# The channel shift of a convolution block by transfers, and two elementwise steps moved from VectorE to ScalarE, in a kernel that follows a table of times

## The chip, the cores and the metric

The kernel runs on one core of a Trainium2 chip. A core has a matrix engine (TensorE, PE in the profile, with its weight loads as PEld), VectorE (DVE), ScalarE (ACT), GpSimd (POOL), and SyncE (SP), which here only issues transfers. The engines run side by side, each through its own queue in order, and wait for each other by semaphores. The metric is the time of one execution on the device in microseconds, as the median of several runs.

## The reference

The input is 64 images of 96 channels and 56 x 56 pixels in float32. Two layers follow each other.

The first is a convolution block. An expansion by a 1x1 convolution to 192 channels, with a batch norm and a silu; a shift of four quarters of the channels by one pixel each, up, left, down and right, with zeros at the edge; a shuffle of the channels; a depthwise 3x3 convolution with batch norms and a scaled identity added; silu; a squeeze-and-excite gate; a projection back to 96 channels; the input added; silu.

```
up, left, down, right = shift of x0, x1, x2, x3 by one pixel
out = shuffle(concat(up, left, down, right))
dw  = depthwise3x3(out)
out = silu(bn(dw + bn(out * id_w)))
```

The second treats each image as 3136 tokens of 96 channels. It adds an attention-like part (layer norm, a matmul to 192 channels with relu, a Fourier transform over the tokens, a complex scale and relu, the inverse transform, a matmul back to 96) and then a feed-forward part (layer norm, then two linear layers whose inputs and weights are rounded to an 8-bit float with 2 bits of mantissa, and whose sums and biases are rounded to a 16-bit float).

## The kernel before

Everything is done image by image, and several images are under way at once. The kernel is a set of small step functions, each of which issues a few instructions: `ea_mm` and `ea_ev` for the expansion of the first 128 channels, `eb_mm` and `eb_ev` for the last 64, `dw_mm`, `gt` and `lt` for the depthwise convolution, `pj_*` for the projection, `c_*` and `sp_*` for the first norm, `w1_*`, `f1_*`, `f2_*`, `w2_*`, `i1_*` and `i2_*` for the Fourier part, `n_*` for the second norm, `x_*`, `h_*` and `o_*` for the feed-forward part, and `x_in`, `f1_st`, `f2_ld`, `i1_st`, `i2_ld` and `o_st` for transfers. The suffix tells the kind: mm a matmul on TensorE, ev its copy out of PSUM, st and ld transfers.

The order of the work is set by hand, by a table. `PLAN` has a time for every step of one image, and `PERIOD` (104.415) is the distance of one image from the next. The steps of all images are sorted by `b * PERIOD + time` and issued in that order (L1021). So the table gives only the order: each engine's queue holds its instructions in that order, and when one really starts depends on its queue and its waits. Part numbers belong to a step: `lt0` to `lt8` are the nine taps.

The shift and the last 64 channels. `xi` holds one image with a border of one pixel, and one more row of ones that carries the bias. For the first 128 channels a quarter is 32 output channels wide, so `ea_mm` reads a window of `xi` that is already shifted (`window`, L394). For the last 64 channels a quarter is only 16 wide. There `eb_mm` (L423) uses weights padded with zeros, `ex_b`, and adds two matmuls of 32 channels in PSUM, one for each shift. The result goes to `e_b`, whose 128 partitions are two halves of the image times 64 channels; four groups have 7 rows in each half and a fifth has the one row that each half needs of the other. `eb_ev` (L439) applies the silu on ScalarE and writes `e_b`. The nine `lt` (L501) then do the depthwise taps of these channels on VectorE, on 1568 elements a partition, and `gt` (L488) does the same for a part of the first 128 channels; TensorE does the rest of these with diagonal weights (`dw_mm`).

The Fourier part and its limits. The matmuls of `w1`, `f1`, `f2`, `w2`, `i1` and `i2` take turns on two PSUM buffers of 1024 columns (`mix_ps`, L385), all other matmuls on four smaller ones (`psb`). `w1_ev` and `f2_s` on VectorE, and `f1_ev`, `f2_u`, `w2_ev` and `i1_ev` on ScalarE, read the large buffers and set when they come free. The spectrum goes through DRAM twice: `f1_st` and `f2_ld`, then `i1_st` and `i2_ld` (L894), each on SP's queue; `i2_mm` (L908) starts when the rows are back.

The second norm: `n_mm` gives the centred values in PSUM, `n_sq` squares them on ScalarE, `n_v` sums on VectorE, `n_pow` takes the inverse root on GpSimd, and `n_x` (L939) multiplies, on VectorE, and writes `xt` as 8-bit floats for `x_mm`. `o_b` (L994) adds the last bias to the 16-bit result in place, on VectorE, and `o_f` on GpSimd adds the residual.

Of the kernel before, what the change touches and what calls it, by code (L numbers as in the profile page):

```python
# [7 lines left out]
F32 = mybir.dt.float32  # L8
F16 = mybir.dt.float16
F8 = mybir.dt.float8e5  # L10
AF = mybir.ActivationFunctionType
# [4 lines left out]
C = 96  # L16
# [29 lines left out]
    "x_in": (-38.1521383, -39.0313507, -38.1421592, -29.5328898, -31.2956739, -49.0488434, -53.4484414),  # L46
    "ea_mm": (12.0718742, -17.6347537, -10.7617034, 21.5633635, 22.3815668, -27.4838656, 20.8444028),
    "ea_ev": (12.7625155, -16.7409792, -10.2350254, 22.8295655, 23.1485054, -26.8731307, 22.1730006),
    "eb_mm": (-24.9502373, -30.5666300, -24.2855462, -28.5828763, -25.9329880),
    "eb_ev": (-24.4007802, -29.0870142, -23.6123341, -27.8995689, -24.6078971),  # L50
    "dw_mm": (23.4012692, 25.8065649, 27.7186515),
    "dw_ev": (27.9416140, 28.2430920, 28.7919300, 27.9867333),
    "gt": (
        23.2893122, 23.6403008, 24.7084475, 26.2430594, 26.9625479, 31.2412715, 31.4805021, 31.6854971, 32.2081696,
    ),
    "gs": (35.5837667,),
    "lt": (
        -22.5058312, -19.2781395, -16.0020596, -8.0830315, -5.6296105, 10.1142041, 11.3886298, 19.2795806, 21.4543236,
    ),
    "ls": (25.2835963,),  # L60
    "se1_mm": (37.8386681,),
    "se1_ev": (39.1563442,),
    "se2_mm": (42.2104890,),
    "se2_ev": (42.5090105,),
    "se2_th": (42.5348385,),
    "se2_pw": (44.5599295,),
    "pj_mm": (49.5318932, 49.8734317, 59.5185874, 59.7120461),
    "pj_add": (56.4058332, 52.4986738, 55.7518604, 50.5578889, 62.0059751, 61.7026537, 60.4028988, 62.1927170),
    "pj_ev": (57.4207106, 54.3789408, 55.8536804, 52.2030223, 63.6733108, 63.8836718, 63.6259052, 62.6258470),
    "c_mm": (64.0752216, 64.2093635, 64.1823953, 67.0833950, 66.7447747, 69.5982071, 72.4532417),  # L70
    "c_st": (65.0824106, 67.4206134, 66.4132179, 72.2682213, 68.2606423, 72.6061913, 77.5871617),
    "c_v": (75.0177019, 80.2993483),
    "c_pow": (76.9880774, 83.3522602),
    "sp_v": (79.7136264, 84.6589124),
    "sp_ld": (81.9540079, 100.3604366),
    "sp_mm": (82.7320710, 85.1331094),
    "sp_ev": (83.1910055, 89.2419308),
    "sp_st": (84.0313823, 91.2838064),
    "w1_mm": (87.1292398, 87.4650255, 98.3635707, 98.4934935, 110.6216463, 107.9122279, 120.0467391, 121.3099629),
    "w1_ev": (88.4753488, 89.6606871, 101.8145979, 102.1457936, 112.1440653, 108.1905137, 121.3097887, 122.6670408),  # L80
    "f1_mm": (92.4329783, 93.9413197, 102.1475205, 103.0182652, 113.5623380, 116.3511041, 124.4090057),
    "f1_ev": (93.7039784, 97.4318585, 105.1183982, 107.7539289, 114.5573476, 117.0384673, 125.0694061),
    "f1_st": (95.0609843, 107.1692695, 108.9817725, 116.6729491, 117.5442084, 123.9939344, 131.9160193),
    "f2_ld": (133.6363282, 134.4630140, 140.6697451, 148.5715304),
    "f2_mm": (134.0425675, 147.3297886, 141.4082867, 149.2531837, 154.9429947, 160.6005067),
    "f2_u": (
        135.7660808, 139.9328971, 150.0014492, 150.1774566, 142.0370395, 143.6677530, 151.8678977, 153.2265284,
        158.0769692, 158.2232886, 163.0150847, 163.7461056,
    ),
    "f2_s": (  # L90
        139.9838717, 141.9248308, 152.1198117, 152.1631925, 146.0651549, 146.9747432, 153.1711643, 153.5938621,
        158.8634913, 158.8771759, 163.4341277, 164.8079993,
    ),
    "f2_r": (144.0109778, 153.5991704, 148.7491184, 156.4744876, 159.5323121, 167.3989389),
    "f2_p": (147.3373312, 156.4376915, 150.8056372, 162.7962275, 161.2485624, 169.6535678),
    "w2_mm": (162.8750213, 159.0401908, 167.8463641, 170.9122124),
    "w2_ev": (166.1738607, 159.3392453, 169.9047276, 172.9202964),
    "i1_mm": (166.2532752, 170.2567201, 173.3466199),
    "i1_ev": (169.8622129, 169.2534145, 172.5737063, 172.7147615, 173.4172382, 175.8838783),
    "i1_st": (176.0044405, 181.5692360, 182.6172474),  # L100
    "i2_ld": (184.2359480, 189.7575058),
    "i2_mm": (189.1909858, 188.5912958, 198.3815920, 196.3644526),
    "i2_ev": (190.1672752, 191.7878315, 189.7544042, 190.0259385, 201.9647931, 201.2712574, 197.5328114, 196.9362029),
    "n_mm": (194.1130474, 192.8787732, 204.8582159, 214.9114818, 204.2743160, 208.7914968, 202.7409001),
    "n_sq": (194.2312052, 193.7168380, 207.3352049, 215.2880641, 204.5888294, 211.0101067, 204.2114539),
    "n_v": (195.8071958, 194.1326641, 207.9103855, 215.6737355, 210.6800138, 211.1668257, 205.1116119),
    "n_pow": (199.0696775, 198.6534423, 208.5806040, 217.6340298, 211.4651491, 211.6665408, 205.2342939),
    "n_x": (200.9444099, 200.0782994, 210.9942246, 218.2272324, 212.2097752, 217.7795795, 206.6554285),
    "x_mm": (202.3277533, 200.8863307, 217.5496343, 219.8683239, 216.0782138, 219.4636355, 207.7029227),
    "x_ev": (203.0727144, 205.8355865, 217.8646967, 220.1867695, 218.5087841, 220.9334171, 210.6012880),  # L110
    "h_mm": (
        222.6648803, 228.7422803, 227.1038383, 222.6083835, 226.7371014, 221.6336581, 240.2108454, 244.1922873,
        250.9628025, 264.7686132, 241.4045277, 261.6477397, 239.3650273, 275.9040589, 273.9147053, 281.5223325,
        289.5279227, 292.6649548, 292.9723382, 304.6785521, 295.5712479,
    ),
    "h_ev": (
        226.6852415, 230.3656128, 228.5097649, 225.3267902, 228.0507042, 222.0383113, 242.5456463, 246.3460033,
        252.6763911, 265.6097590, 254.2998624, 262.5612295, 246.1430109, 277.5023560, 275.1846881, 283.9585886,
        293.1805221, 293.5958189, 301.7720564, 306.3205803, 300.5311760,
    ),  # L120
    "h_b": (
        227.9255047, 233.9060669, 232.2385810, 225.3989664, 230.2401387, 225.1796682, 244.0448546, 246.4021124,
        262.6890256, 267.2414236, 271.8809825, 274.9000227, 256.1324325, 278.4500149, 275.7375432, 293.7448928,
        297.6207746, 299.0605055, 302.8303038, 319.7169921, 312.2914909,
    ),
# [14 lines left out]
def conv_attn_ffn(  # L140
# [98 lines left out]
    for e in range(2):  # L239
        nc.vector.tensor_copy(  # L240
            ex_b[:, e, :, e, :], ex_w[:, 128:MID].rearrange("p (u e i) -> p u e i", u=2, e=2)[:, :, e, :]
        )
# [956 lines left out]
```

## Time and profile before

| | |
|---|---|
| median of 3 runs | 6730.21 us (6729.68 to 6732.37) |
| the profiled execution | 6725.7 us |
| its span, first to last instruction | 6723.9 us |
| PE busy | 6152.3 us, 91% |
| VectorE busy | 5639.2 us, 84% |
| ScalarE busy | 4384.5 us, 65% |
| GpSimd busy | 1493.4 us, 22% |
| mean granted TensorE clock | 0.986 |
| moved by DMA | 689.44 MB, 103 GB/s |

A row of a group reads: line, engine, operation, names of output and inputs, shapes, count, then the busy time in us and the mean of one in ns, then the time that the engine stood idle just before it and what ended that. A matmul in float32 shows as two records. A row of a timeline reads: start, length, engine, line, operation, and in brackets the idle time before it. A row of an SP timeline shows only the issue of a transfer, not its landing. A row of the table of windows has the window, its length, the busy time and count of each engine, the granted clock, the share of the DMA engines and GB/s.

### The profile page before, as it was taken

To read this page: it belongs to the slowest core of one execution; us is meant where nothing else is said; L and a number is where in the kernel's file an instruction comes from. 1 tells how busy PE (TensorE), PEld (TensorE's weight loads), DVE (VectorE), ACT (ScalarE), POOL (GpSimd) and SP (SyncE) were. 2 spreads that over 40 slices of the span, in tenths; PEclk is the share of its full clock that TensorE was granted. 3 is DMA by queue.
4 is the path that set the end of the run, shared out by engine and by line. 5 is a ranking of instruction groups with operands and counts; after the bars stand their busy time and mean duration, and the time that the engine had idled before them with its cause. 6 is when DMAs were issued, how large, how long until landed. Compare 5 with 4: busy or idle time off the path is not lost.

```text
span 6723.9 us, 246864 instructions
## 1 busy us (share of the span) xinstructions
PE 6152.3 (91%) x107010; PEld 4033.1 (60%) x107010; DVE 5639.2 (84%) x10903; ACT 4384.5 (65%) x8718; POOL 1493.4 (22%) x1035
## 2 busy tenths in 40 slices
PE   6999999999999999999999999999999999999996
PEld 3656655666656666566566666666665656656654
DVE  7888888888888888888888888888888888888884
ACT  2666666666666666666666666666666666666665
POOL 1212212222222222122222222221222222212212
PEclk9999999999999999999999999999999999999997
DMA  3344444344444444443444444444434444444333
GB/s 76 99 104 106 103 104 105 101 102 109 103 103 105 106 104 103 104 109 98 102 109 103 103 104 106 104 103 104 108 100 103 107 103 103 105 103 108 101 96 82
DMA packets 996378, 689.44 MB, mean 103 GB/s; under 512 B 671298, under 2 KB 944522, under 8 KB 995162
## 3 DMA queue, kind: packets, MB, share of 16 engines
q1 hardware_dynamic: 992570, 671.88, 39.1%
q8 instruction: 841, 13.78, 0.9%
q10 hardware_dynamic: 2720, 1.77, 0.1%
q14 instruction: 247, 2.02, 0.1%
HBM read 329.66 MB, written 341.31 MB: 100 GB/s over the span
## 4 chain that ended last, share of the span: by engine, by line
PE 43%; DVE 35%; ACT 12%; DMA 4%; issue 4%; POOL 1%; SPq 1%; POOLq 0%; ACTq 0%; DVEq 0%
PE ps_d L475 10%; DVE ue L813 6%; DVE buf_h L823 5%; DVE s L810 5%; PE psa L873 5%; ACT ue L794 4%; PE ps_ea L413 4%; PE psa L696 4%; PE ps_eb L430 4%; DVE buf_h L708 3%; DVE d_last L509 3%; PE psa L723 3%; DMA buf_h<-rows 3%; PE ps_c L626 3%; DVE y L974 3%
## 5 line engine op out<-in xcount | busy, mean ns | idle before, releaser
L1002 POOL TENSOR_TENSOR o<-t,o 112x448 f32<-112x448 f32 x448 | 688.7, 1537 | 3539.8 <-DVE o L996 1277.9
L509 DVE SCALAR_TENSOR_TENSOR d_last<-e_b,taps,d_last 128x1568 f32<-128x1568 f32 x512 | 1008.6, 1970 | 2.6
L980 ACT CAST h<-y 128x448 fp8e5<-128x448 f16 x1344 | 747.7, 565 | 167.9 <-DVE y L974 167.8
L496 DVE SCALAR_TENSOR_TENSOR d_vec<-e_a,taps,d_vec 128x1120 f32<-128x1120 f32 x512 | 766.1, 1496 | 13.9
L969 ACT CAST y<-ps_h 128x448 f16<-128x448 f32 x1344 | 692.0, 542 | 90.2 <-PE ps_h L964 79.9
L475 PE MATMUL ps_d<-e_a,diag 32*32 32x504 f32 x18432 | 710.6, 590 | 17.0 <-issue 16.9
L936 POOL TENSOR_TENSOR rs<-v,mhalf 112x4 f32<-112x4 f32 x448 | 450.0, 1012 | 1193.0 <-DVE v L620 1193.0
L696 PE MATMUL psa<-w1c,t 112*64 112x96 f32 x14336 | 652.5, 247 | 1.4 <-ACT fs L735 1.4
L696 PEld LDWEIGHTS psa<-w1c,t 112*64 112x64 f32 x14336 | 607.2, 137 | 73.7 <-DVE t L920 35.9
L794 ACT ACTIVATE ue<-psa,fa 128x448 f32<-128x448 f32 (+1 forms) x512 | 358.9, 704 | 381.3 <-DVE ue L813 355.8
L634 DVE BATCH_NORM_STATS2 st<-ps_c 112x6 f32<-112x96 f32 x1792 | 336.3, 249 | 313.4 <-PE ps_c L626 313.4
L475 PEld LDWEIGHTS ps_d<-e_a,diag 32*32 32x32 f32 x18432 | 392.0, 103 | 325.1 <-issue 69.8
L974 DVE TENSOR_SCALAR y<-y,qb 128x448 f16<-128x448 f16 x1344 | 510.2, 384 | 69.1 <-ACT y L969 65.2
L964 PE MATMUL ps_h<-xq,q 96*128 96x448 fp8e5 x1344 | 425.1, 359 | 131.2 <-ACT t L600 109.3
L769 PEld LDWEIGHTS psa<-l_tab,buf_g 128*64 128x64 f32 x7424 | 361.5, 137 | 241.1 <-issue 109.4
L615 ACT ACTIVATE sq<-ps_n 112x384 f32<-112x384 f32 x448 | 220.2, 492 | 430.6 <-PE ps_n L608 430.2
L769 PE MATMUL psa<-l_tab,buf_g 128*64 128x112 f32 x7424 | 414.6, 263 | 83.8 <-DVE ue L813 46.2
L834 PEld LDWEIGHTS psa<-w2a,buf_h 128*64 128x64 f32 (+1 forms) x7424 | 331.8, 135 | 218.8 <-issue 172.2
L653 POOL TENSOR_TENSOR rs<-v,mhalf 112x16 f32<-112x16 f32 (+1 forms) x128 | 338.0, 2640 | 494.0 <-DVE v L648 494.0
L723 PE MATMUL psa<-buf_h,f_tab 56*64 56x384 f32 x3584 | 401.6, 504 | 47.6 <-DVE buf_h L708 46.8
L810 DVE SCALAR_TENSOR_TENSOR s<-psa,fa,ue 128x448 f32<-128x448 f32 (+1 forms) x512 | 325.1, 635 | 137.3 <-ACT ue L794 137.2
L708 DVE SCALAR_TENSOR_TENSOR buf_h<-psa,rs_full 128x768 f32<-128x768 f32 (+1 forms) x512 | 424.8, 850 | 10.2 <-PE psa L696 9.0
(175 smaller groups left out, 12093.1 us busy)
## 6 DMA issues: line engine op xcount, KB each, us to landing
spec<-fs SPq DMA_DIRECT2D x896, 192.0 KB
buf_g<-spec SPq DMA_DIRECT2D x384, 336.0 KB
buf_h<-rows SPq DMA_DIRECT2D x128, 672.0 KB
x<-in_x SPq DMA_DIRECT2D x896, 84.0 KB
out_dram<-o SPq DMA_DIRECT2D x896, 84.0 KB
rows<-buf_g SPq DMA_DIRECT2D x128, 420.0 KB
rows<-buf_g SPq DMA_DIRECT2D x64, 504.0 KB
buf_g<-spec SPq DMA_DIRECT2D x128, 210.0 KB
```

Source lines behind the costliest of these rows:

```text
L475: nc.tensor.matmul(pss[r][j * 32 : j * 32 + 32], lhsT=diag[pr, tap, :], rhs=e_a[pr, r0 : r0 + SR, dx : dx + HW], start=tap == 0, stop=tap ...
L496: nc.vector.scalar_tensor_tensor(d_vec, win, w, d_vec, ALU.mult, ALU.add)
L509: nc.vector.scalar_tensor_tensor(d_last, win, w, d_last, ALU.mult, ALU.add)
L696: nc.tensor.matmul(ps[hc * 64 : hc * 64 + 64, k, 0:C], lhsT=t[:, n0 : n0 + 64], rhs=w1c[:, hc * C : hc * C + C], start=True, stop=True,)
L708: nc.vector.scalar_tensor_tensor(h_v[:, d * NJ + j0 : d * NJ + j0 + n, :], ps[:, 0:n, 0:C], 0.0, rs_full[:, d, j0 : j0 + n].unsqueeze(2).t ...
L769: nc.tensor.matmul(ps[c0 : c0 + 64, k, 0:CP], lhsT=g_v[:, k1, c0 : c0 + 64], rhs=l_tab[:, k1, :], start=True, stop=True,)
L794: nc.scalar.activation(held["ue", b, i][:, q, 0:n, :], held["f2", b, i][:, 0:n, 0:HW], AF.Identity, bias=par[:, 2 + q : 3 + q], scale=par[ ...
L810: nc.vector.scalar_tensor_tensor(held["s", b, i][:, q, 0:n, :], im, par[:, m : m + 1], a, ALU.mult, ALU.add)
L969: nc.scalar.copy(y16, held.pop(("h", b, i)))
L974: nc.vector.tensor_scalar(y16, y16, qb1[:, i % 3 : i % 3 + 1], 0.0, ALU.add, ALU.max)
L980: nc.scalar.copy(held["h8", b, j][:, m, :], held.pop(("y", b, i)), saturate=False)
L1002: nc.gpsimd.tensor_tensor(o32, rows, o16, ALU.add)
```

## The change

Three things change in the work, and the table of times is a new one throughout (PERIOD stays).

1. The last 64 channels. `ex_b` goes. `eb_mm` now multiplies the unshifted image by the plain weights, 64 channels at once, for each of the two halves; four groups of 8, 8, 7 and 7 rows cover 30 rows of each half, border rows included. `eb_ev` writes the silu of it to a new buffer `e_u`. A new step `eb_sh` copies 16 channels with their shift from `e_u` into `e_b`: two transfers for each of the four quarters, on SP's queue. Where the shift is up or down a transfer moves whole rows, one run a partition; where it is left or right it moves 29 rows of 55 elements a partition.
2. `n_x` is four activations on ScalarE (a copy with a scale from a column), one for each 96 columns, in place of one multiplication on VectorE.
3. `o_b` is an activation with a bias on ScalarE.

In the new table, `eb_sh` stands after the last row load and the `sp_ld` of the same image period, and all nine `lt` stand after `eb_sh`; before, `lt0` to `lt4` stood among the transfers of the rows, the first `i2_ev` and the first `w1_ev`.

```diff
-    EB = (((0, HH), 7), ((7, HH + 7), 7), ((14, HH + 14), 7), ((21, HH + 21), 7), ((HH, HH - 1), 1))
+    EB = ((0, 8), (8, 8), (16, 7), (23, 7))
     def eb_mm(b, i):
...
-        for e in range(2):
-            for h in range(2):
-                for u in range(2):
-                    p0 = h * 64 + u * 32
-                    nc.tensor.matmul(
-                        ps[p0 : p0 + 32],
-                        lhsT=ex_b[:, e, u].rearrange("p e i -> p (e i)"),
-                        rhs=window(2 * u + e, rows[h], n),
-                        start=e == 0,
-                        stop=e == 1,
-                    )
+        for h in range(2):
+            r1 = 1 + h * (HH - 2) + r0
+            nc.tensor.matmul(
+                ps[h * 64 : h * 64 + 64],
+                lhsT=ex_w[:, 128:MID],
+                rhs=xi[:, r1 : r1 + n, 1 : HW + 1],
+                start=True,
+                stop=True,
+            )
...
+        nc.scalar.activation(e_u[:, r0 : r0 + n, 1 : HW + 1], held.pop(("eb", b, i)), AF.Silu)
+
+    def eb_sh(b, q):
+        dy, dx = SHIFT[q][0] - 1, SHIFT[q][1] - 1
+        for h in range(2):
+            pr = slice(h * 64 + q * 16, h * 64 + q * 16 + 16)
...
+            nc.sync.dma_start(
+                out=e_b[pr, y0 + to : y1 + to + 1, x0 + 1 : x1 + 1],
+                in_=e_u[pr, y0 + at : y1 + at + 1, x0 + dx + 1 : x1 + dx + 1],
+            )
...
     def n_x(b, g):
...
-        nc.vector.tensor_tensor(
-            xt, cen[:, :, 0:C], rs.unsqueeze(2).to_broadcast([CP, 4, C]), ALU.mult, saturate=False
-        )
+        for k in range(4):
+            nc.scalar.activation(xt[:, k, :], cen[:, k, 0:C], AF.Copy, scale=rs[:, k : k + 1], saturate=False)
...
     def o_b(b, j):
...
-        nc.vector.tensor_scalar(o16, o16, qb2, None, ALU.add)
+        nc.scalar.activation(o16, o16, AF.Identity, bias=qb2)
```

The part of the table that places the shifted channels:

```diff
+    "eb_sh": (-8.8730867, -8.2956889, -9.2075340, -8.4273685),
...
     "lt": (
-        -22.5058312, -19.2781395, -16.0020596, -8.0830315, -5.6296105, 10.1142041, 11.3886298, 19.2795806, 21.4543236,
+        -0.5489800, 3.2067798, 7.4056550, 9.3934270, 10.2124864, 17.5519195, 22.1593808, 25.4801538, 25.8145632,
```

## The prediction

> **What bounds the kernel now.** The page's busy line comes first:
>
> ```profile
> PE 6152.3 (91%) x107010; PEld 4033.1 (60%) x107010; DVE 5639.2 (84%) x10903; ACT 4384.5 (65%) x8718; POOL 1493.4 (22%) x1035
> ```
>
> TensorE leads and VectorE is close behind. An average hides when each is full, so the next view is the table of windows over one image in mid-run. I cut it at the first inverse matmul (L908) that follows the transfer of the inverse rows, at the end of the depthwise matmuls (L475), and where the frequency stage ends:
>
> ```profile
> 3277.05:3325.28 48.23, 46.78 (x997) 30.98 (x999) 46.73 (x67) 27.99 (x56) 13.07 (x11) 1.00 0.41 103
> 3325.28:3359.00 33.72, 29.44 (x433) 20.21 (x432) 29.43 (x50) 26.37 (x50) 3.91 (x3) 0.95 0.32 80
> 3359.00:3380.07 21.07, 20.63 (x245) 11.79 (x245) 11.47 (x55) 14.08 (x33) 6.49 (x3) 1.00 0.56 145
> ```
>
> The columns after the length are PE, PEld, DVE, ACT and POOL busy. In the first 48 us PE and DVE are both full; in the middle 34 us neither is, and they wait for each other through the two psa buffers; in the last 21 us PE alone is full and DVE idles half. One image takes 103.0 us, PE works 96.8 of it. A faster engine pays only where it is last in its stretch. The timelines of PE and VectorE then show the joints:
>
> ```profile
> 3318.98 9.42 DVE L496 SCALAR_TENSOR_TENSOR d_vec<-e_a,taps,d_vec 128x1120 f32<-128x1120 f32 x6
> 3329.73 0.68 DVE L810 SCALAR_TENSOR_TENSOR s<-psa,fa,ue 128x448 f32<-128x448 f32 x1 [0.29 <-ACT ue L794]
> 3380.07 2.12 PE L908 MATMUL psa<-r_tab,buf_h 64*48 64x56 f32 x96 [0.32 <-DMA buf_h<-rows]
> ```
>
> Call the start of L908 t0 (3277.05, then 3380.07). Part A is t0 to the first f2_s (L810): 3329.73 - 3277.05 = 52.7 us. Part B is from there to the next t0: 50.3 us. L908 itself waits 0.32 us for a transfer, which the timeline of the SP queue explains:
>
> ```profile
> 3367.97 3.85 SPq L892 DMA_DIRECT2D rows<-buf_g  x2
> 3375.02 0.39 SPq L898 DMA_DIRECT2D buf_h<-rows  x1
> 3375.46 3.25 SPq L664 DMA_DIRECT2D rs_full<-rs  x4
> 3379.30 0.59 SPq L683 DMA_DIRECT2D t<-dev_t  x1
> 3380.05 0.65 SPq L897 DMA_DIRECT2D probe<-buf_h  x1
> 3380.74 0.39 SPq L898 DMA_DIRECT2D buf_h<-rows  x1
> ```
>
> From the last L873 (ends 3370.50) to L908 there are 9.6 us of copy, store and load, and PE fills them with other work, the e_b matmuls among it.
>
> **The change, part by part.** The rows for the costs:
>
> ```profile
> L509 DVE SCALAR_TENSOR_TENSOR d_last<-e_b,taps,d_last 128x1568 f32<-128x1568 f32 x512 | 1008.6, 1970 | 2.6
> L496 DVE SCALAR_TENSOR_TENSOR d_vec<-e_a,taps,d_vec 128x1120 f32<-128x1120 f32 x512 | 766.1, 1496 | 13.9
> L980 ACT CAST h<-y 128x448 fp8e5<-128x448 f16 x1344 | 747.7, 565 | 167.9 <-DVE y L974 167.8
> L430 PE MATMUL ps_eb<-x,ex_b 112*32 112x392 f32 x4096 | 367.0, 497 | 2.0 <-DMA x<-in_x 2.0
> L942 DVE TENSOR_TENSOR xt<-ps_n,rs 112x384 fp8e5<-112x384 f32 x448 | 241.0, 550 | 21.6 <-POOL rs L936 21.2 <-PE psa L696 0.3
> L996 DVE TENSOR_SCALAR o<-o,qb 112x448 f16<-112x448 f16 x448 | 146.1, 326 | 10.1 <-ACT o L991 10.1
> L677 ACT COPY dev_t<-ps_dev 16x112 f32<-16x112 f32 x64 | 15.1, 236 | 1.9 <-PE ps_dev L671 1.9
> ```
>
> *Matmuls.* 40 calls an image become 8. On the PE timeline the old ones take 2.84 + 3.02 = 5.86 us (4 groups of two rounds at 0.69, and the halo rows). A new group is one round: two 64-column calls side by side, 392 or 448 columns, 0.69 or 0.80 us by L430 and L413; four are 3.0. PE loses 2.86 us, 96.85 to 94.0. These matmuls stand in the 9.6 us hidden behind the transfer, so PE alone doesn't collect it there; the new table moves two more ea groups in, and I sum 10.3 us of PE work between the last L873 and L908.
>
> *The shifts.* Eight transfers an image join SP's queue, after the second row load and the last four rs_full. Four have 16 runs of 6.7 KB, four have 464 runs of 220 B. In SP order: load issued at t0+1.1; rs_full waits for the power on POOL, about t0+2.1, and takes 3.3 to 3.9, so t0+6; eight issues at 0.59 to 0.76 (the SBUF-to-SBUF rows above and L664) end at t0+11 to +12. Landing isn't shown for such a form. Near row: L892 issued by 3371.8 lets L898 go at 3375.02, 3.2 us. Here a rule matters: the Trainium skill, "DMA: Bandwidth & Descriptors", Specifications, says that transfers under 512 B fall below line rate, while its section "Why small descriptors are slow (HBM only)" exempts SBUF to SBUF. The trace's mean packet takes 39.1% x 16 x 6723.9 / 992570 = 42 ns (677 B); 116 short ones per DMA engine, if spread over all 16, are 4.9 us, from t0+9. By the exemption they'd be half, and landing is issue plus 2. So all eight have landed at t0+13.5 to t0+18; I take t0+15, and twice the row's packet time for a bad end, t0+20. Behind them on SP wait one dev_t store and the first spec stores, used 5 and 20 us later: nothing.
>
> *Who waits for the shifts.* lt0 (L507). Before, lt0 to lt4 used VectorE's idle time around t0; now all nine lt start after the landing. Behind lt0 in VectorE's queue stands w1_ev, which frees a psa buffer for TensorE. From lt0 to the last gt the queue holds 9 lt (1.06 + 8 x 1.97), 9 gt (0.80 + 8 x 1.50), 6 w1_ev (4.9), 4 n_v (2.9), 9 h_b (3.5): 40.9 us, less 0.08 overlap for each of some 39 instructions (seen where one row starts before the last ends) = 37.7. One w1_ev finds its matmul 1.3 us late. Part A becomes 15 + 37.7 + 1.3 = 54.0, against 52.7: the shift costs 1.3 here, because the lt left their cover.
>
> *n_x to ScalarE.* VectorE loses 7 x 0.55 = 3.9 us an image. ScalarE gains 28 activations of 96 columns. Row L677 (112 columns from PSUM) has 0.236 alone, about 0.15 behind another: 4.2 to 6.6 us. The Trainium skill, "ScalarE: Activation LUTs", Rules for kernel authors, speaks against it: multiply and add belong on VectorE, and an ACTIVATE is about 0.3 us + 0.83 ns an element, 0.38 each, 10.6 us. By rule a group is 1.5 us, by row 0.7; I take the row, a copy of the same kind. An n_x waits for POOL's power; behind it stand f1_ev and x_ev, which free psa and psb. VectorE's old wait there was 21.2 us in all, 0.05 a group. By the row nothing is late; by the rule two groups run into x_mm, +1.5 us.
>
> *o_b to ScalarE.* VectorE loses 7 x 0.33 = 2.3, ScalarE gains 7 x 0.565 = 4.0 (L980's form). It waits for nothing, and o_f comes 9 us or more later in the table. Hidden; without slack 0.5 us each. ScalarE's total: 68.4 + 4.2 to 10.6 + 4.0 - 0.3 (four e_u evictions for six) = 76 to 83 of 100: not the bound.
>
> *Part B.* Following the new order: f2_s up to the ninth and tenth halves ends 18.5 us after f2_s0 (8 x 1.28, 2 x 1.18, f2_p 3.3, pw and gate 0.9, pj_add 1.2, h_b 0.25), PE short work to 19.5, then w2 2.3, f2 1.1, L873 1.75, projection 3.2, w2 2.3 and 1.6, L873 1.6, transposes 1.5, L873 1.6: 36.5. Then 10.3 of hidden-transfer filler: 46.8, against 50.3. The gain of 3.5 is less PE work in line (L873 and a w2 group stand earlier) and VectorE freed of two o_b and the c_st.
>
> *Sum.* 54.0 + 46.8 = 100.8 an image, -2.2. The first and last L512 are 6440.0 us apart, 102.2 an image; 62 full images give -136. The table ends its last store 10 us later after the depthwise stage, some +5 at the end. Span 6723.9 - 131 = 6593. The profiled execution took 6725.7, the median is 6730.2, 6.3 over the span: **6599 us**.
>
> **The rivals.** (1) Everything hides: landing at t0+13, no stall, period 98: 6730 - 62 x 5 = 6420. For it: PE 94.0 and VectorE 82 would allow it; against: six us of PE idle have been there before. Chance 0.14. (2) Slower: the 220 B transfers land late. Each us past t0+17.2 is lost, since lt0 heads VectorE's full stretch; t0+20 is +2.8 x 62 = +170: 6905, at t0+18.5 6810. Chance 0.20. (3) ScalarE's queue blocks TensorE in the n stage, by the rule's price and POOL's turns, +3.5 us an image: 100.8 + 3.5 = 104.3: 6810. Chance 0.13. (4) The saving is given back: 6730. Chance 0.07, 0.05 of it within 0.2% (13 us, about what a measurement here can tell). The likeliest has 0.46.
>
> **The numbers.** Faster 0.46 + 0.14 + 0.01 = 0.61; same 0.05; slower 0.20 + 0.13 + 0.01 = 0.34. The likeliest's own range is 6500 to 6690 (landing 2 us either way, stalls 1). Eight in ten takes in most of (1) and most of the slower cases: 6430 to 6840.
>
> **What would show it.** PE busy about 5970; ps_eb near 3 us an image; VectorE near 5240 (5639 less 64 x 6.2). Right: lt0 (its new line) waits for a DMA about 1.5 us an image. Wrong: that wait is over 4 us, or x_mm and f1 wait for ScalarE by more than 2 us an image, or the 6.3 us of PE idle grow past 9.

## The result, and the profile after

The changed kernel takes 6877.8 us (median of 4 runs, 6870.3 to 6882.8) where the kernel before takes 6729.9 (6726.5 to 6732.4): the ratio is 1.0219, 95% interval 1.0201 to 1.0237. The forecast was 6599. The page of the changed kernel, its busy line:

```profile
PE 6094.7 (89%) x102914; PEld 4018.3 (58%) x102914; DVE 5310.4 (77%) x10004; ACT 4977.8 (72%) x10830; POOL 1557.3 (23%) x1036
```

TensorE lost 58 us of work where the forecast had 183, VectorE lost 329 where it had some 400, ScalarE gained 593. In the span of 6881.0 us TensorE now idles 786 us, before 572. The table of windows over one image, cut at t0, at lt0, at the first f2_s and at the next t0 (length, then PE, PEld, DVE, ACT and POOL busy, granted clock, DMA share, GB/s):

```profile
3356.11:3371.16 15.05, 14.54 (x431) 13.50 (x431) 9.29 (x21) 10.74 (x28) 6.43 (x5) 1.00 0.63 117
3371.16:3410.93 39.77, 33.29 (x592) 18.91 (x587) 38.53 (x42) 28.92 (x70) 11.32 (x7) 1.00 0.48 118
3410.93:3461.77 50.84, 48.55 (x593) 31.69 (x593) 34.36 (x95) 37.83 (x73) 7.65 (x5) 0.90 0.41 101
```

Ahead of lt0 VectorE has 5.8 us of idle time, where the kernel before has some of its lt. From lt0 to the first f2_s it is full: 38.5 of 39.8 us. The joints in the timelines of VectorE and TensorE:

```profile
3371.16 1.04 DVE L507 TENSOR_SCALAR d_last<-e_b,taps 128x1568 f32<-128x1568 f32 x1 [1.56 <-DMA t<-dev_t]
...
3409.63 1.38 DVE L496 SCALAR_TENSOR_TENSOR d_vec<-e_a,taps,d_vec 128x1120 f32<-128x1120 f32 x1
3410.93 0.68 DVE L810 SCALAR_TENSOR_TENSOR s<-psa,fa,ue 128x448 f32<-128x448 f32 x1
```

```profile
3356.11 2.08 PE L908 MATMUL psa<-r_tab,buf_h 64*48 64x56 f32 x94
...
3461.77 2.52 PE L908 MATMUL psa<-r_tab,buf_h 64*48 64x56 f32 x112
```

The first f2_s (L810) follows the last gt (L496) with no gap, so the end of VectorE's full stretch is the start of the f2 stage. SP's timeline shows why the stretch starts where it does:

```profile
3358.46 3.24 SPq L664 DMA_DIRECT2D rs_full<-rs  x4
3361.74 6.43 SPq L445 DMA_DIRECT2D e_b<-e_u  x8
3368.28 0.91 SPq L683 DMA_DIRECT2D t<-dev_t  x1
3369.88 6.24 SPq L744 DMA_DIRECT2D spec<-fs  x4
```

The eight shifts are issued from 5.6 to 12.1 us after t0, and lt0 starts at t0+15.05. And the groups that the prediction's steps need:

```profile
L509 DVE SCALAR_TENSOR_TENSOR d_last<-e_b,taps,d_last 128x1568 f32<-128x1568 f32 x512 | 1085.8, 2121 | 2.4
L496 DVE SCALAR_TENSOR_TENSOR d_vec<-e_a,taps,d_vec 128x1120 f32<-128x1120 f32 x512 | 704.7, 1376 | 2.6
L769 PE MATMUL psa<-l_tab,buf_g 128*64 128x112 f32 x7424 | 470.6, 285 | 138.7 <-DMA buf_g<-spec 124.6 <-DVE ue L813 11.9 <-DVE pw L559 2.1
L943 ACT ACTIVATE xt<-ps_n,rs 112x96 fp8e5<-112x96 f32 x1792 | 458.3, 355 | 92.4 <-POOL rs L936 87.5
L810 DVE SCALAR_TENSOR_TENSOR s<-psa,fa,ue 128x448 f32<-128x448 f32 (+1 forms) x512 | 325.3, 635 | 314.6 <-ACT ue L794 314.6
L995 ACT ACTIVATE o<-o,qb 112x448 f16<-112x448 f16 x448 | 291.5, 665 | 0.1
L422 PE MATMUL ps_eb<-x,ex_w 112*64 112x392 f32 (+1 forms) x1024 | 213.5, 533 | 4.5 <-DMA x<-in_x 4.5
L507 DVE TENSOR_SCALAR d_last<-e_b,taps 128x1568 f32<-128x1568 f32 x64 | 66.4, 1037 | 161.3 <-DMA t<-dev_t 93.8 <-DMA e_b<-e_u 44.5 <-DMA spec<-fs 22.8
```

L507 is lt0: it waits 161.3 us in all for transfers, 2.5 us an image. The transfer named last differs (dev_t, e_b, spec), but all three are issued on SP around the shifts, and of these lt0 reads only `e_b`. The same line of the kernel before:

```profile
L507 DVE TENSOR_SCALAR d_last<-e_b,taps 128x1568 f32<-128x1568 f32 x64 | 67.6, 1057 | 140.8 <-ACT e_b L443 140.8
```

There lt0 waits almost as long, for ScalarE, but ahead of t0, with the first lt in VectorE's idle time. So the wait alone says little; what counts is what stands behind it in VectorE's queue.

One image is one sample, so from here on A, B and the image are means over 38 images in mid-run (the 13th to the 50th), worked out from the starts in each trace, with t0, A (t0 to the first f2_s) and B (from there to the next t0) as the prediction has them. All in us; the last column is the median of the timed runs.

| kernel | lt0 after t0 | A | B | image | time |
|---|---|---|---|---|---|
| before | -1.75 | 52.24 | 50.48 | 102.71 | 6730 |
| changed | 15.90 | 55.84 | 48.94 | 104.77 | 6878 |

A is 3.6 us longer, B only 1.5 shorter.

Where lt0's 15.9 us go can be read from the DMA packets that the trace of the changed kernel also holds; packets of 220 B belong to the shifts alone. In the mean over the same 38 images the first shift is issued at t0+5.7, the last issue ends at t0+12.4, the last packet of 220 B ends at t0+15.1, and lt0 starts 0.8 us after it.

### The profile page after: what moved, and what is told of

Its sections match the earlier page's. It is cut to its first block, busy times and chain, and to the rows that moved or that the text cites. A ratio compares the mean times of both kernels' runs of the same rounds, so it can differ in the third digit from the quotient of the medians.

```text
span 6881.0 us, 241042 instructions
## 1 busy us (share of the span) xinstructions
PE 6094.7 (89%) x102914; PEld 4018.3 (58%) x102914; DVE 5310.4 (77%) x10004; ACT 4977.8 (72%) x10830; POOL 1557.3 (23%) x1036
## 5 line engine op out<-in xcount | busy, mean ns | idle before, releaser
L1001 POOL TENSOR_TENSOR o<-t,o 112x448 f32<-112x448 f32 x448 | 640.9, 1431 | 3392.2 <-DMA out_dram<-o 2566.2
L509 DVE SCALAR_TENSOR_TENSOR d_last<-e_b,taps,d_last 128x1568 f32<-128x1568 f32 x512 | 1085.8, 2121 | 2.4
L936 POOL TENSOR_TENSOR rs<-v,mhalf 112x4 f32<-112x4 f32 x448 | 553.0, 1238 | 827.4 <-DVE v L620 811.4
L696 PE MATMUL psa<-w1c,t 112*64 112x96 f32 x14336 | 692.1, 248 | 46.8 <-DMA t<-dev_t 26.4
L496 DVE SCALAR_TENSOR_TENSOR d_vec<-e_a,taps,d_vec 128x1120 f32<-128x1120 f32 x512 | 704.7, 1376 | 2.6
L475 PE MATMUL ps_d<-e_a,diag 32*32 32x504 f32 x18432 | 617.2, 590 | 13.9 <-ACT e_a L412 13.2
L769 PEld LDWEIGHTS psa<-l_tab,buf_g 128*64 128x64 f32 x7424 | 412.8, 151 | 323.9 <-issue 231.1
L769 PE MATMUL psa<-l_tab,buf_g 128*64 128x112 f32 x7424 | 470.6, 285 | 138.7 <-DMA buf_g<-spec 124.6
L810 DVE SCALAR_TENSOR_TENSOR s<-psa,fa,ue 128x448 f32<-128x448 f32 (+1 forms) x512 | 325.3, 635 | 314.6 <-ACT ue L794 314.6
L943 ACT ACTIVATE xt<-ps_n,rs 112x96 fp8e5<-112x96 f32 x1792 | 458.3, 355 | 92.4 <-POOL rs L936 87.5
L973 DVE TENSOR_SCALAR y<-y,qb 128x448 f16<-128x448 f16 x1344 | 463.6, 353 | 71.5 <-ACT y L968 69.5
L735 ACT COPY fs<-psa 128x768 f32<-128x768 f32 x448 | 370.6, 827 | 171.5 <-PE psa L723 167.2
L723 PE MATMUL psa<-buf_h,f_tab 56*64 56x384 f32 x3584 | 409.9, 520 | 80.7 <-DVE buf_h L708 77.7
```

What stands on the lines that cost most here:

```text
L475: nc.tensor.matmul(pss[r][j * 32 : j * 32 + 32], lhsT=diag[pr, tap, :], rhs=e_a[pr, r0 : r0 + SR, dx : dx + HW], start=tap == 0, stop=tap ...
L496: nc.vector.scalar_tensor_tensor(d_vec, win, w, d_vec, ALU.mult, ALU.add)
L509: nc.vector.scalar_tensor_tensor(d_last, win, w, d_last, ALU.mult, ALU.add)
L696: nc.tensor.matmul(ps[hc * 64 : hc * 64 + 64, k, 0:C], lhsT=t[:, n0 : n0 + 64], rhs=w1c[:, hc * C : hc * C + C], start=True, stop=True,)
L769: nc.tensor.matmul(ps[c0 : c0 + 64, k, 0:CP], lhsT=g_v[:, k1, c0 : c0 + 64], rhs=l_tab[:, k1, :], start=True, stop=True,)
L936: nc.gpsimd.tensor_tensor(rs, held.pop(("nv", b, g)), mhalf[0:CP, 0:4], ALU.pow)
```

## The experiments

Names that begin with a_ keep the new table, names with b_ the old one. Three theories fell, in whole or in part, before one held; they are told in their order (the numbers 2 and 3 were rivals of the first). Ratios are to the kernel before on the same chip, with 95% intervals. Differences in us are between medians; the kernel before itself had medians from 6716 to 6737 us from chip to chip.

### One part of the change undone at a time

Theory 1 was that the late lt fill VectorE up to the f2 stage, and that the spectrum's round trip through DRAM and a halved TensorE clock follow from it. Rivals: ScalarE's added work (1), the new order as a whole (2), the added DMA traffic (3). The edits put back the lines of the diff above: `a_nx_dve` the multiplication on VectorE, `a_ob_dve` the bias on VectorE, `a_eb_mm` the old `ex_b`, `EB`, `eb_mm` and `eb_ev` without `eb_sh`, `a_table_only` all three.

```diff
     # a_eb_mm: five groups again, in the new table; no eb_sh
-    "eb_mm": (-25.0746307, -24.8668402, -31.0126563, -29.6079375),
-    "eb_ev": (-24.8115274, -23.7696889, -27.1911807, -26.7446361),
+    "eb_mm": (-25.0746307, -24.8668402, -31.0126563, -29.6079375, -24.9500000),
+    "eb_ev": (-24.8115274, -23.7696889, -27.1911807, -26.7446361, -23.7000000),
```

> The changed kernel (6878 us) with the normalised values written by VectorE again, one instruction a group in place of four on ScalarE; table and all else as changed. Theory 1 (the nine lt stand so late that they fill VectorE up to the f2 stage; the spectrum's round trip through DRAM and a half clock follow): ScalarE loses 7 x 1.04 = 7.3 us an image and VectorE gains 7 x 0.5 = 3.5 us, both away from the stretch in question: 6850 to 6900 us. Rival 1 (ScalarE's added work is what costs): 2 us or more an image come back, 6750 us or less. Rival 2 (the new order alone) and rival 3 (the added DMA traffic): no change, 6870 to 6890 us.

> The changed kernel with the last bias added by VectorE again (7 x 0.3 us an image there, 7 x 0.665 us less on ScalarE); table and all else as changed. Theory 1 (late lt): 6860 to 6895 us. Rival 1 (ScalarE's load): 1 us an image or more comes back, 6810 us or less. Rivals 2 (order) and 3 (traffic): 6870 to 6890 us.

> The changed kernel with the shift of the last 64 channels made by matmuls again (five groups, no transfers within SBUF), in the new table, the nine lt at the changed kernel's late places. TensorE gets 2.6 us an image more, the eight transfers and lt0's wait (2.5 us an image) go. Theory 1 (it is the place of the lt in VectorE's order that costs, not the transfers themselves): 6830 to 6910 us. Rival 3 (the added traffic slows the spectrum's transfers): 6750 us or less. Rival 1 (ScalarE) and rival 2 (order): 6860 to 7040 us, up to 62 x 2.6 = 160 us slower.

> All three parts undone: the work of the kernel before in the new table of times, with the nine lt at the changed kernel's late places. Theory 1 (late lt) and rival 2 (the order, in whatever place): still slow, 6830 to 6950 us. Rival 1 (ScalarE) and rival 3 (traffic): the time of the kernel before or near it, 6700 to 6780 us.

| kernel | lt0 after t0 | A | B | image | time | ratio |
|---|---|---|---|---|---|---|
| a_nx_dve | 15.71 | 61.39 | 48.45 | 109.84 | 7191 | 1.0688 (1.0663 to 1.0714) |
| a_ob_dve | 16.23 | 56.62 | 48.88 | 105.50 | 6921 | 1.0293 (1.0276 to 1.0311) |
| a_eb_mm | 13.44 | 53.38 | 50.88 | 104.25 | 6819 | 1.0137 (1.0120 to 1.0154) |
| a_table_only | 14.36 | 60.07 | 51.17 | 111.24 | 7253 | 1.0786 (1.0769 to 1.0803) |

Rival 1 is out for this order: both ScalarE parts gain there, 313 and 43 us. How much n_x gains was a surprise, and no theory had it. The groups of a_nx_dve, then the matmuls of the kernel before:

```profile
L951 PE MATMUL ps_x<-eye,xt 112*96 112x112 fp8e5 x1792 | 181.3, 237 | 302.6 <-DVE xt L942 295.2 <-ACT fs L735 1.0 <-ACT xq L958 0.6
L951 PEld LDWEIGHTS <-xt 112*96 112x96 fp8e5 x1792 | 126.8, 135 | 392.0 <-DVE xt L942 382.3 <-issue 2.0
```

```profile
L951 PE MATMUL ps_x<-eye,xt 112*96 112x112 fp8e5 x1792 | 151.2, 219 | 34.3 <-DVE xt L942 34.3
```

TensorE's matmuls wait 295.2 / 64 = 4.6 us an image for xt, before 0.5: n_x stands in VectorE's queue among the late lt. (The weight loads wait in the same time; the two waits overlap and must not be added.) a_table_only also misses its range, by 300 us, and has the same wait (285.4 us in all), so the old work in the new order doesn't tell what the order alone costs. The shift's row is the telling one: without transfers lt0 comes 2.46 us earlier and A is 2.46 shorter, while B grows by 1.94, because TensorE has its 2.6 us of ps_eb again. The net is small, 59 us.

### The lt moved, the round trip, the clock

`a_eb_mm_lt` moves the lt of a_eb_mm to where the kernel before has them. `a_stale` and `b_stale` read another image's spectrum. `a_fill` puts idle matmuls on TensorE into the wait.

```diff
     # a_eb_mm_lt
-        -0.5489800, 3.2067798, 7.4056550, 9.3934270, 10.2124864, 17.5519195, 22.1593808, 25.4801538, 25.8145632,
+        -17.4, -16.6, -14.8, -6.5, -3.4, 8.6, 9.4, 21.9, 22.16,
     # a_stale, b_stale
-                out=g_v[r * 64 : r * 64 + HW, k0:k1, :], in_=held["spec", b][:, r * 32 + k0 : r * 32 + k1, :]
+                out=g_v[r * 64 : r * 64 + HW, k0:k1, :], in_=held["spec", max(b - 1, 0)][:, r * 32 + k0 : r * 32 + k1, :]
     # a_fill, in f2_mm ahead of the real matmuls
+        if i in (0, 2):
+            for k in range(12 if i == 0 else 20):
+                for c0 in (0, 64):
+                    nc.tensor.matmul(ps[c0 : c0 + 64, k % 8, 0:CP], lhsT=g_v[:, k % 8, c0 : c0 + 64],
+                                     rhs=l_tab[:, k % 8, :], start=True, stop=True)
```

> The kernel with the shift by matmuls in the new table (6819 us), with nothing but the nine lt moved in VectorE's order to where the kernel before has them: two ahead of the i2 stage, one after its first half, two after its second, two after the middle w1_ev, two after the last w1_ev; the rest of the table as changed. Theory 1 (late lt fill VectorE up to the f2 stage): the w1_ev come 4 us or more earlier, and the spectrum with them: 6550 to 6740 us. Rival 2 (the new order as a whole): 6790 to 6850 us. Rivals 1 and 3: no change from 6819 us.

> The changed kernel (6878 us), with the load of the spectrum reading the previous image's spectrum in DRAM, so that it doesn't wait for this image's last store to land; the output is then another one, all work and all transfers stay. Theory 1 as to its end (the round trip through DRAM is exposed, 2.6 us an image of TensorE's wait, and the half clock follows on it): the loads go some 3.5 us earlier, 6640 to 6800 us. If the round trip is covered by other work: 6860 to 6880 us.

> The kernel before (6730 us) with the same edit: the spectrum's load reads the previous image's spectrum. TensorE's waits for that load are 32 us in all there. Theory 1: at most that comes back, 6690 to 6735 us. If the round trip costs the kernel before as much as the changed one (so that it explains no difference): 6600 us or less.

> The changed kernel with idle matmuls added on TensorE ahead of the first and the second group of the f2 stage (24 and 40, some 3.5 us an image in all), into PSUM that the real ones then overwrite; they read a quarter of the spectrum that has landed. If the half clock after the idle is a part of the loss (3.26 in place of 1.75 us for two groups of the f2 stage, up to 3 us an image): the clock holds and 50 to 180 us come back, 6700 to 6830 us. If the clock's fall lies in time that TensorE would wait anyway, or the idle is not its cause: 6860 to 7000 us.

| kernel | lt0 after t0 | A | B | image | time | ratio |
|---|---|---|---|---|---|---|
| a_eb_mm_lt | -0.10 | 53.74 | 52.55 | 106.28 | 6956 | 1.0323 (1.0308 to 1.0339) |
| a_stale | 16.00 | 56.54 | 47.74 | 104.28 | 6851 | 1.0171 (1.0156 to 1.0186) |
| b_stale | -1.71 | 52.53 | 50.40 | 102.93 | 6749 | 1.0021 (1.0012 to 1.0029) |
| a_fill | 15.85 | 58.53 | 50.82 | 109.35 | 7154 | 1.0611 (1.0594 to 1.0629) |

Theory 1's chain of effects falls. Taking the wait for the last store away brings back about 30 us of 148, not 80 or more (in the kernel before the same edit cost 13 us; why stays open). Moving the lt alone made the kernel slower by some 130 us: two lt ahead of the i2 stage now hold i2_ev, which comes 2.81 us after t0 in place of 1.48, and the f2 stage starts no earlier. Most of the loss lies in B: the stretch from the first f2_s to the end of the tenth half takes 23.08 us in place of 21.36. Why wasn't tried. a_fill settles nothing about what the clock costs. In the image shown it did keep the clock up: with the idle matmuls (the 4.08 and 4.05 us of L768) ahead of them, both groups of f2 (L779) run in 1.7 us, in the timeline of TensorE:

```profile
3551.98 4.08 PE L768 MATMUL psa<-l_tab,buf_g 128*64 128x112 f32 x48 [0.70 <-DMA buf_g<-spec]
3555.89 1.71 PE L779 MATMUL psa<-l_tab,buf_g 128*64 128x112 f32 x32
...
3559.49 4.05 PE L768 MATMUL psa<-l_tab,buf_g 128*64 128x112 f32 x80
3563.38 1.70 PE L779 MATMUL psa<-l_tab,buf_g 128*64 128x112 f32 x32
```

But the filler took 8.1 us an image, not the 3.5 that I had reckoned with (a float32 matmul is two records), which is more than fits into the wait.

### Two chains into the f2 stage

Theory 4 read off these traces that two chains meet in the f2 stage (VectorE's stretch, and the last f1 with the spectrum behind it), and moved the ends of both in the new table. The steps that move, by name, with their times in the table modulo PERIOD:

```
a_w1_early, and with it a_w1_gt and a_eb_mm_lt_w1 (there w1_ev7 and w1_ev6 go to 15.05 and 15.06; f1_ev5, f1_ev6, f1_st5 and f1_st6 follow their f1)
-    w1_mm6 19.21, w1_mm7 21.20, w1_ev7 21.78, w1_ev6 21.85, f1_mm5 16.51, f1_mm6 23.59, f2_ld0 28.86
+    w1_mm6 14.14, w1_mm7 14.15, w1_ev7 17.30, w1_ev6 17.35, f1_mm5 12.20, f1_mm6 17.50, f2_ld0 18.20
a_gt_late, and with it a_w1_gt (the gates' other steps follow)
-    gt7 34.65, gt8 35.85, gs 36.98, se1_mm 39.81, se2_mm 40.86, se2_pw 45.74
+    gt7 40.00, gt8 40.10, gs 40.20, se1_mm 44.00, se2_mm 45.00, se2_pw 47.60
```

> The changed kernel (6878 us) with nothing but the end of the w1 and f1 stages moved forward in the table: the last two w1_mm ahead of three ea_mm on TensorE, the last two w1_ev ahead of lt5 and gt0 on VectorE, the last two f1 and their stores behind them. Theory 4, formed from the runs before (two chains meet in the f2 stage: the second f2_u comes 19.5 to 20.1 us after the last f1_ev in the kernel before, in the changed one and in the four made from it without altered f2, and the first f2_s comes when the last gt is done; in the changed kernel the first chain ends 1.7 us behind the second): only the first chain is shortened, so 1 to 2 us an image come back: 6750 to 6830 us. If the last f1_ev alone sets the period: 3 us an image or more, 6700 us or less. If neither does: 6860 to 6890 us.

> The changed kernel with the last two gt moved behind the first two f2_s on VectorE (into the wait for the second group of the f2 stage), and gs and the gates behind them by 3 to 4 us. Theory 4: only VectorE's chain is shortened, by 2.75 us, and the spectrum's still ends where it did: 6850 to 6890 us. If VectorE's stretch from lt0 to the last gt alone sets the period: 2.75 us an image come back, 6690 to 6730 us.

> The changed kernel with both of these moves. Theory 4: both chains are shortened, by some 2.7 to 3.5 us an image: 6640 to 6740 us, more than the sum of the two moves alone. If the two chains don't bind together: the sum of what the two moves bring alone.

> The kernel with the shift by matmuls and the nine lt where the kernel before has them, in the new table (6956 us), with the end of the w1 and f1 stages moved forward as well. Theory 4: in the 6956 us VectorE was no longer full, and the last f1_ev came no earlier because TensorE's order held it; moved forward, 3 us an image or more come back: 6600 to 6780 us. If the last f1_ev doesn't set the period there: 6930 to 6980 us.

Measured: 7118, 7032, 7344 and 7192 us (ratios 1.0599, 1.0468, 1.0939 and 1.0704, each to 0.002). All four miss by far, and on the wrong side. Each of the two moves put a wait at the head of another queue. In a_w1_early the depthwise matmuls wait for the expansion, which now stands behind w1; its group, and that of the changed kernel after it:

```profile
L475 PE MATMUL ps_d<-e_a,diag 32*32 32x504 f32 x18432 | 727.7, 674 | 139.1 <-ACT e_a L412 116.6 <-issue 22.0
```

```profile
L475 PE MATMUL ps_d<-e_a,diag 32*32 32x504 f32 x18432 | 617.2, 590 | 13.9 <-ACT e_a L412 13.2 <-issue 0.7
```

A becomes 60.95. In a_gt_late A is shorter, 54.96, but TensorE then waits at the gates' first matmul (L519: 126.1 us, changed kernel 25.5) with the f2 stage behind it, and B is 52.41. So theory 4 isn't shown, nor is its contrary: an order with these moves would need the rest of the table to be moved with them.

### One part alone, in the old order

Theory 5: the shift costs through the late lt in any order, the other two parts gain a little. The first two edits are those of the diff; for the shift alone the old table got the transfers and as much of a move of the lt as they need.

```diff
     # b_sh, and with all three parts b_all
+    "eb_sh": (-19.01, -19.00, -19.03, -19.02),
-        -22.5058312, -19.2781395, -16.0020596, -8.0830315, -5.6296105, 10.1142041, 11.3886298, 19.2795806, 21.4543236,
+        -8.0830315, -5.6296105, -2.1, 10.1142041, 11.3886298, 12.5, 19.2795806, 21.4543236, 21.5,
```

> The kernel before (6720 to 6735 us) in its own order, with the normalised values alone written by ScalarE (four instructions a group). Theory 5 (of the three parts, the shift by transfers costs through the late lt, and the other two gain a little or nothing in any order, as they did in the new one, where undoing them cost 313 and 43 us): 6640 to 6740 us. Rival (in an order not made for it, ScalarE's 7.3 us an image stand in its queue ahead of what TensorE waits for in the n stage): 6790 us or more.

> The kernel before in its own order, with the last bias alone added by ScalarE. Theory 5: 6700 to 6740 us. Rival (ScalarE's queue): 6760 us or more.

> The kernel before in its own order, with the shift of the last 64 channels alone by transfers: eight transfers on SP behind the second half of the i2 load, and as much of the order moved as that needs, so that the first lt stands where the fourth stood (10 us after the first i2_ev) and three lt come among the later ones. Theory 5 (the three lt moved into VectorE's fuller stretch put the f2 stage off by 3 us or more, TensorE's 2.8 us come back behind it): 6710 to 6850 us. If the late lt don't cost: 6550 to 6600 us.

> The kernel before in its own order with all three parts, lt as in the run with the shift alone: the changed kernel's work without its table. Theory 5 (the parts, not the table): within 60 us of the changed kernel's 6878 us or better, 6650 to 6900 us. If the new table is needed for the new division of the work: 7000 us or more.

| kernel | lt0 after t0 | A | B | image | time | ratio |
|---|---|---|---|---|---|---|
| b_nx_act | -1.50 | 54.69 | 50.13 | 104.82 | 6893 | 1.0247 (1.0231 to 1.0262) |
| b_ob_act | -1.94 | 52.13 | 49.96 | 102.09 | 6701 | 0.9963 (0.9948 to 0.9977) |
| b_sh | 12.78 | 57.05 | 50.19 | 107.24 | 7017 | 1.0428 (1.0411 to 1.0446) |
| b_all | 12.29 | 57.55 | 49.52 | 107.06 | 7018 | 1.0434 (1.0419 to 1.0450) |

The bias alone on ScalarE, in the old order, is faster than the kernel before, by 25 us or 0.37%. Theory 5 is wrong on n_x: in the old order it costs 167 us, so its worth depends on the order. In b_nx_act the squares of the next group stand behind n_x in ScalarE's queue, and VectorE waits for them (211.6 of the 274.4 us below fall where the square starts right behind an n_x); the group of b_nx_act, then of the kernel before:

```profile
L619 DVE TENSOR_REDUCE v<-sq 112x4 f32<-112x384 f32 x448 | 246.6, 550 | 275.2 <-ACT sq L615 274.4 <-POOL rs L936 0.3
```

```profile
L619 DVE TENSOR_REDUCE v<-sq 112x4 f32<-112x384 f32 x448 | 244.0, 545 | 13.1 <-ACT sq L615 11.3
```

On top of the shift, n_x and o_b then cost nothing more (b_all and b_sh differ by 2 us). The shift alone makes A 4.8 us longer than before. And TensorE's saving doesn't come back in B, because in the old order i2_mm then waits for its rows; the group of b_sh:

```profile
L911 PE MATMUL psa<-r_tab,buf_h 64*48 64x56 f32 x14336 | 381.9, 225 | 165.5 <-DMA buf_h<-rows 161.2 <-DVE v L622 2.6 <-DVE y L977 1.0
```

From the last i1_mm (L873 in the kernel before) to t0 there are still 9.27 us, of which TensorE works 6.92; before it was 9.70 with 9.24.

### The transfers kept, the waiting for them taken away

Theory 6: what costs is that the lt come after the landing. Both kernels keep all eight transfers and let the lt read `e_u`, so that nothing waits for them (the taps then come from unshifted channels).

```diff
     # a_unshifted; b_sh_unshifted also has the nine lt at the old table's times
-        win = e_b[:, dy : dy + HH, dx : dx + HW]
+        win = e_u[:, dy : dy + HH, dx : dx + HW]
```

> The run with the shift alone in the old order (7017 us), with the nine lt back at their old places and reading the expanded values where ScalarE writes them, not the shifted copy: nothing waits for the transfers, which still run; the taps of the last 64 channels are then taken from unshifted channels, so the output is another one. Theory 6 (what costs is that the lt come after the transfers: the first part of the image, to the fifth f2_s, is 58.8 us there and 53.9 before): the first part is 54 us again, the rest 48.4 as in that run: 6690 to 6760 us. If it is the eight transfers themselves, on SP's queue or in the memory traffic: 6930 us or more.

> The changed kernel (6878 us) with the nine lt at their places, reading the expanded values and not the shifted copy, so that lt0 waits for no transfer, and the transfers still run; the output is another one. Theory 6: lt0 starts some 2.5 us earlier, as in the run with the shift by matmuls (11.9 us after the first i2_ev in place of 14.4), VectorE's full stretch and the f2 stage with it, and the rest of the image stays 46.0 us: 6690 to 6760 us. If the landing isn't what holds the image back: 6840 to 6880 us.

| kernel | lt0 after t0 | A | B | image | time | ratio |
|---|---|---|---|---|---|---|
| b_sh_unshifted | -3.72 | 53.33 | 50.22 | 103.55 | 6784 | 1.0079 (1.0062 to 1.0096) |
| a_unshifted | 13.67 | 53.81 | 48.74 | 102.54 | 6727 | 0.9999 (0.9990 to 1.0007) |

This holds. In the new order lt0 comes 2.23 us earlier and the image is 2.23 shorter: from lt0 to the next t0 both kernels take 88.87 us. All of the 148 us are gone. The groups of a_unshifted:

```profile
L507 DVE TENSOR_SCALAR d_last<-e_u,taps 128x1568 f32<-128x1568 f32 x64 | 66.0, 1031 | 6.4 <-ACT e_u L433 6.4
L769 PE MATMUL psa<-l_tab,buf_g 128*64 128x112 f32 x7424 | 478.1, 288 | 129.4 <-DMA buf_g<-spec 118.1 <-DVE ue L813 8.9 <-ACT s L817 2.2
L810 DVE SCALAR_TENSOR_TENSOR s<-psa,fa,ue 128x448 f32<-128x448 f32 (+1 forms) x512 | 325.1, 635 | 305.6 <-ACT ue L794 305.6
```

L507 no longer waits. L769 and L810 look as bad as in the changed kernel: the wait for the spectrum (118.1 against 124.6 us), the slow f2 matmuls (288 against 285 ns), VectorE's waits for f2_u. All that I had first taken for causes is still there, in a kernel that takes the time of the one before. So none of it makes the 148 us; whether it keeps back the gain that was forecast is another matter, and the next section comes to it. In the old order 233 of 290 us go, with lt0 back in VectorE's idle time (here the places of the lt and the waiting change together); the 57 that stay are 24 beyond the expected range. A is still 1.1 us longer than before and i2_mm still waits for its rows; how the 57 us divide wasn't tried.

What the transfers themselves cost, on SP and in the memory traffic, isn't told apart from TensorE's saving by these two runs. a_eb_mm sets a bound: it has the same order but for the eb steps and none of the shifts' transfers, nothing waits for such a transfer in either kernel, and a_unshifted takes 92 us less (6727 against 6819), 1.9 us an image from lt0 to the next t0. The transfers running by themselves cost less than TensorE's 2.6 us an image bring.

## Why the prediction was wrong

| step of the prediction | predicted | measured |
|---|---|---|
| lt0 after t0 | 15 | 15.90 |
| lt0 to the first f2_s | 37.7 + 1.3 = 39.0 | 38.52 busy + 1.42 idle = 39.94 |
| Part A | 54.0 | 55.84 |
| first f2_s to the tenth half done | 18.5 | 21.79 |
| from there to the last L873 | 18.0 | 16.98 |
| last L873 to t0 | 10.3 | 10.17 |
| Part B | 46.8 | 48.94 |
| image | 100.8 | 104.77 |

**The matmuls: right.** ps_eb takes 213.5 / 64 = 3.3 us an image (3.0 predicted, 5.9 before), and the stretch hidden behind the rows' transfer is 10.17 us of which TensorE works 10.06 (10.3 summed).

**Who waits for the shifts: right in kind, too small in size.** The mechanism is the one that the prediction gives: lt0 waits for the landing and heads a stretch of 38 to 40 us in which VectorE is full. A was to grow by 1.3 us and grew by 3.6. Two terms were 0.9 us too small each, the landing and VectorE's busy time in the stretch (38.5, not 37.7; by the rows of L509 and L496 an lt takes 2.12 us, not 1.97, and a gt 1.38, not 1.50), and the forecast started from one image with an A of 52.7 where the mean is 52.24.

The landing came near its 15 us in part by luck. Issue ended at t0+12.4, a little later than the t0+11 to t0+12 foretold. A packet of 220 B took 22.7 ns of a DMA engine, and not the 42 of the trace's mean packet; per byte that is about what the shifts' long packets take (6.5 and 6.7 KB in 606 and 735 ns). So the exemption for transfers within SBUF that the prediction cites agrees with this trace, though the half that was reckoned for it was a guess. But the landing was not "issue plus 2": the last packet ended 2.7 us after the last issue, and lt0 started another 0.8 us later. What fills these 3.5 us isn't known.

**Part B: the step that failed.** The prediction summed the f2 stage by VectorE's instructions alone, 18.5 us (the terms that it lists make 18.25), and put at nothing VectorE's waits for f2_u, which ScalarE does. The sum of the work was right: in the changed kernel VectorE is busy for 18.40 us between the first f2_s and the end of the tenth half (an f2_s does one half of a group, twelve in an image). But this stretch takes 21.79 us, and 3.03 of the rest are waits for f2_u. In the kernel before it takes 21.40, 18.85 of them busy and 2.44 in such waits, and in none of the twenty kernels run here is it under 20.66. The group of the kernel before, for the row of L810 above (both kinds of f2_s together wait 200.8 us in all before and 350.1 after):

```profile
L810 DVE SCALAR_TENSOR_TENSOR s<-psa,fa,ue 128x448 f32<-128x448 f32 (+1 forms) x512 | 325.1, 635 | 137.3 <-ACT ue L794 137.2
```

The 18.5 were then set against Part B of the kernel before as measured, waits and all. So of the 3.5 us of gain in B, 2.9 were time that had been left out of one side only. What B really gained is 1.5 us: 2.4 in the work from the tenth half to the last L873, less 0.4 in the f2 stage and 0.5 in front of t0. What sets the pace of f2_u in this stage stays open.

**The sum.** The image took 104.77 us and not 100.8. Of these 4.0 us, 3.3 are the f2 stage, 0.9 the landing and 0.9 VectorE's stretch; 1.1 went the other way, almost all of it because the work behind the tenth half had been priced 1.0 us too high.

**n_x and o_b.** n_x takes ScalarE 458.3 / 64 = 7.2 us an image, between the row's 4.2 to 6.6 and the rule's 10.6; o_b takes 0.665 us, not 0.565. ScalarE's total, 77.8 us an image, is in the range given. The matmuls of x_mm wait 63.4 / 64 = 1.0 us an image for it (1.7 with the weight loads), under the mark of 2, and those of f1 (L723) wait for VectorE. In this order rival (3) didn't come. In the old order n_x on ScalarE did cost 167 us, but the wait that stands out there is VectorE's (274.4 us for the squares), where rival (3) has TensorE's.

**The marks.** Of those set for "wrong", TensorE's idle time past 9 us an image came true (10.2); lt0's wait, 2.5 us, stayed under 4. VectorE's busy time, 5310.4, missed the 5240 foretold, and TensorE's, 6094.7, missed the 5970. The f2 matmuls of L769 alone took 56 us more than before (470.6 us, before 414.6), at a lower granted clock (0.968 in the mean of the run, before 0.986); the rest isn't broken down. The group of the kernel before:

```profile
L769 PE MATMUL psa<-l_tab,buf_g 128*64 128x112 f32 x7424 | 414.6, 263 | 83.8 <-DVE ue L813 46.2
```

**Rival (2) is nearest to what happened.** It said that each microsecond of late landing is lost, and a_unshifted shows just that rate: 2.23 us of lt0 for 2.23 us of image. Its turning point was wrong. It had the loss begin at t0+17.2; the runs show the kernel level with the one before at t0+13.7, because the gain in B that was to pay for the rest wasn't there.

Open: shifts from another queue, or fewer of them, which might end the 6.7 us of issue sooner, weren't tried. Also open is what the half clock costs by itself.

## What to carry to other kernels

Cost both sides of a comparison in the same way: a sum of busy times for the new order may only be set against the same sum for the old one, and a stretch whose sum misses the measured time of the kernel before isn't ready to forecast the kernel after. When work is put behind a transfer, look at where it stood: work that filled an engine's idle time for nothing can become work in a full stretch, and here the landing's delay then counted one to one. What an engine's move is worth belongs to the order around it: n_x on ScalarE lost 167 us in one order and gained 313 in the other.

## What the runs showed of the hardware

An activation of 96 columns from PSUM with its scale from a column takes 355 ns (L943), and a group of four 458.3 / 448 = 1.02 us, so each adds about 0.22 us to the one before it. I had priced it by row L677, a copy without such an operand, and by a rule of thumb. The Trainium skill, "ScalarE: Activation LUTs", has a closer price in its section "What ACT_TABLE_LOAD costs": 186 ns with immediates, 93 more for each operand from a column, 0.833 ns an element, and 93 ns of overlap back to back. That makes 359 ns alone and 1.16 us for four as an estimate (the last three at 266); the trace's 1.02 is a little better. For o_b it gives 280 + 0.833 x 448 = 653 ns, where the trace has 665.

In the middle of the changed kernel TensorE's granted clock fell to half in a stretch that followed one of little TensorE work (3.44 of 7.50 us), as two windows show, with two rows of TensorE's timeline from them:

```profile
3404.00:3411.50 7.50, 3.44 (x39) 2.14 (x38) 7.46 (x9) 6.93 (x17) 0.00 (x0) 0.95 0.47 117
3411.50:3420.00 8.50, 8.42 (x122) 7.46 (x122) 5.61 (x11) 6.27 (x13) 1.30 (x1) 0.50 0.35 86
```

```profile
3405.78 1.75 PE L769 MATMUL psa<-l_tab,buf_g 128*64 128x112 f32 x32
3411.58 3.26 PE L769 MATMUL psa<-l_tab,buf_g 128*64 128x112 f32 x32 [2.08 <-DMA buf_g<-spec]
```

The same group of f2 matmuls takes 3.26 us in place of 1.75. It looks like the cause of the loss, and isn't what sets the changed kernel off from the one before: a_unshifted has the same slow matmuls (288 against 285 ns) and doesn't wait for the shifts, and it takes no more than the kernel before. Whether it keeps back a part of the gain that was forecast isn't shown.
